# A fused graph layer on one core: a gate weight load issued later, row-sorting loads cut by row half, and two weight transforms in other batches

## The chip, the core and the metric

The kernel runs on one core of one Trainium2 chip, in float32. The time is the device time of one execution in microseconds (us); the figure given is the median of several executions. Engines are called PE (TensorE, matrix products and transposes), DVE (VectorE), ACT (ScalarE), POOL (GpSimd) and SP (SyncE, which only issues DMAs here). A DMA is issued by SP, ACT or POOL, each with a queue of its own, and moved by 16 DMA engines that all queues share.

## The reference

One layer of a graph network on 32 batches of 512 nodes with 256 features. With h = relu(layernorm(x)):

```python
h1 = relu(bn1(conv1(h)))                      # 1x1 convolution
x_conv = relu(bn2(conv2(h1)) + h)             # 17 taps along the nodes
s = h @ w_se.T + b_se                         # 3 columns
A = exp(-|s_n - s_m|^2) * adj                 # 512 x 512 for each batch
x_nmp = A @ relu(h @ w_msg.T + b_msg)
gi = concat(x_conv, x_nmp) @ w_ih.T + b_ih
gh = h @ w_hh.T + b_hh
r, z = sigmoid(gi_r + gh_r), sigmoid(gi_z + gh_z)
n = tanh(gi_n + r * gh_n)
out = x + (1 - z) * n + z * h
```

## The kernel before, in words

The 17-tap convolution is done in the frequency domain: the nodes of a batch are cut into windows of 64, transformed to 80 rows (40 "units" of two rows), multiplied by transformed weights, and turned back. A window transform serves 16 batches at once, so the 32 batches are two groups of 16, and the work comes in five stages in order of time:

1. the first part of group 0 (0 to 158 us): normalise, transpose, 1x1 convolution and window transform of batches 0 to 15, and in between the transform of the convolution's weights;
2. the nodes of group 0 (158 to 433): affinities, messages and aggregation, and the products of units 0 to 35;
3. the first part of group 1 (433 to 550): batches 16 to 31, with the four left-over units 36 to 39 of group 0 fitted in at its start;
4. the nodes of group 1 (550 to about 821);
5. the gates of all batches, in pairs (from 829).

The order inside a stage is written out by hand: each engine runs its instructions, and each queue issues its DMAs, in the program's order, so an instruction that waits holds all that stands behind it on the same engine. Buffers come from pools, and a load into a buffer waits until the last reader of the earlier content is done. PSUM has 8 banks used in turn.

What the change and the prediction's steps touch:

- `load_rows` (L196 to 199) loads a weight matrix of 256 rows so that partition 32g + i holds the rows 64g + i and 64g + 32 + i. It serves w1 (`load_w1`, into a buffer of 8 rows of which it uses 2), the message weights `wmsg` (256 columns, and 3 columns of the embedding `w_seT`), and two of the three gate weight matrices. It issues four DMAs of 32 partitions.
- `load_x` (L201) loads one batch of x, 512 KB. In `first_part` (L1126 on) batch b + 3 is loaded at the start of batch b's turn, by SP for the first three and by POOL from the fourth on. Three buffers.
- `statistics` (L375 to 381): mean and variance by DVE, then rstd by a power on POOL. `normalise` (L394 on DVE, L392 on ACT for one batch): xn. `transpose_h`: xn to PSUM by PE (L402, called phT), to hT by DVE (L406) with relu, and a store to DRAM by SP (L407, hd). `conv1`: PE (L422, pc), DVE (L425), ACT (L426). `windows_to_freq`: PE (L437, px), ACT copies (L440).
- Weights of the convolution: `load_taps` (L333, L334) loads an eighth of the taps in five DMAs; two buffers. There are 32 steps `weights_to_freq`, four for each eighth. One step is four groups of matmuls (L346, pw), each into a bank of its own, copies of them by ACT (L356) and DVE (L354), and after every second step four stores by SP (L360, wd). `between(b)` hands out the steps to the slots of each batch: n of them in batch b, at most three. Batch 0 has 2, batch 1 none, batches 6 and 11 three, all others two. The first stands after the transposes, the second after the 1x1 convolution, a third after the window transform. The load of the next eighth is put in front of the second step of each even batch from 2 to 12, on POOL, and it can start only when the eighth two places earlier is used up.
- `load_vectors` (L236) and `vectors` (L242 to 254): the bias and normalisation vectors, loaded in batch 5 and worked on by POOL in batch 6.
- The left-over units (L1408 to 1412). `prepare` loads a unit's weights if they are not there (L448, wt, 512 KB) and has POOL add up their two rows (L453, wsum) and the two rows of the factor (L466, both); `product` multiplies (L486, py), the third product needing wsum and both. The list `left` holds five lists of steps, and `first_part` runs one of them at each of its first five calls of `fill()`, among the work for batches 16 to 18. In the second list stands `combine.pop(0)`, which is the load of w_hh (768 KB, by `load_rows` on POOL's queue).
- `combine_weights` adds up the gate weights; its further steps run one in each batch from batch 18 on (`between` of group 1), the first arithmetic on w_hh at 460.60. The load of w_ih's columns for the convolved features goes through `load_rows` on SP's queue at 492.

Of the kernel before, what the change touches and what calls it, by code (L numbers as in the profile page):

```python
# [15 lines left out]
P = 128  # L16
# [134 lines left out]
def gnn_layer(  # L151
# [15 lines left out]
    nc = tc.nc  # L167
# [4 lines left out]
    DC = D // P  # L172
    NC = N // P
    G = 3 * D
    W = N // V
    GB = P // W
# [16 lines left out]
    X, ADJ, XN, HT, HQ, H1, MSG, A, NMP, ST, SL, SR = ({} for _ in range(12))  # L193
    XP, HP, NP, CP, YT, RZ, NT, OUT, AT, TS, MS = ({} for _ in range(11))

    def load_rows(dst, src, queue):  # L196

        for g in range(4):
            queue.dma_start(dst[32 * g : 32 * (g + 1)], src[64 * g : 64 * (g + 1)].rearrange("(e i) o -> i e o", e=DC))

    def load_x(b, queue=nc.sync):  # L201
        X[b] = pools["ahead" if b == GB else "first"].tile([P, NC, D], FP, tag="x", name=f"x_{b}", bufs=1 if b == GB else 3)
# [18 lines left out]
    at, cols, n = {}, {}, 0  # L221
# [1023 lines left out]
    @contextmanager  # L1245
    def phase(*names, bufs=1):
        with ExitStack() as stack:
            for name in names:
                pools[name] = stack.enter_context(tc.tile_pool(name=name, bufs=bufs, reuse_waits="tile"))
            yield  # L1250

    with tc.tile_pool(name="freq", bufs=1) as fpool:
        def freq_tile(g):
            return fpool.tile([P, DC, L, P], FP, tag="xf", name=f"xf_{g}")

        with phase("first", "gen"):
            gen = pools["gen"]
            per = N // D
            steps = [partial(weights_to_freq, gen, pc, i) for pc in range(QI // PI) for i in range(0, PI, per)]

            X[0] = pools["first"].tile([P, NC, D], FP, tag="x", name="x_0", bufs=3)
            for queue, c0, c1 in ((nc.sync, 0, 1), (nc.scalar, 1, 2), (nc.sync, 2, NC)):
                queue.dma_start(X[0][:, c0:c1, :], x[0, c0 * P : c1 * P, :].rearrange("(c p) d -> p c d", p=P))
            load_w1()
            load_x(1)
            load_taps(gen, 0, nc.sync)
            nc.sync.dma_start(taps, nc.inline_tensor(taps_np, name="dft_taps").ap())
            nc.sync.dma_start(fwd, nc.inline_tensor(fwd_np, name="dft_fwd").ap())

            def between(b):  # L1270
                if 1 <= b <= len(load_weights):
                    load_weights[b - 1]()

                n = (2, 0, *(3 if b in (6, 11) else 2 for b in range(2, GB)))[b]
                mine = [[steps.pop(0)] for _ in range(n)]
                if b % 2 == 0 and b // 2 + 1 < QI // PI:
                    mine[b > 0].insert(0, partial(load_taps, gen, b // 2 + 1))
                return (mine[0], mine[1:]) if b == 0 else mine

            with tc.manual_schedule():  # L1280
                xf = first_part(0, freq_tile, between)


        LEFT = 4

        def nodes(g, xf, units, last, following=()):


            b1 = (g + 1) * GB
            pw = pools["pw"]  # L1290
            todo = [b1 - 1, b1 - 2] + list(range(g * GB, b1 - 2))
            loads = [u for u in (*units, *following) if (g, u) not in WT]
            stores = []

            def load_units(n):
                for _ in range(n):
                    if loads:
                        load_unit(g, loads.pop(0))

            def flush():  # L1300
                while stores:
                    stores.pop(0)()

            def multiply(u):
                flush()
                product(pw, g, u, xf, stores)
                if u + 2 in units:
                    prepare(pw, g, u + 2, xf)
                load_units(1)

            load_adj(todo[0], 0)
            load_units(3 - sum((g, u) in WT for u in units))
            message(todo[0])
            load_adj(todo[1], 1)
            load_h(todo[3])
            features(todo[0])
            for step in message_sums(todo[0]):
                step()
            message(todo[1], [0])
            factors(todo[0])  # L1320
            by_chunks(todo[2])
            message(todo[1], [1])
            features(todo[1])
            exponents(todo[0])
            turn(todo[0], [0, 1])
            masked(todo[0], [0, 1])
            turn(todo[0], [2, 3])
            masked(todo[0], [2, 3])
            prepare(pw, g, units[1], xf)
            for step in affinity_sums(todo[0]):  # L1330
                step()
            for i, b in enumerate(todo):
                mine = spread(units, i, last) if i < last else []
                more = todo[i + 1 : i + 5]
                seven = i <= last

                def bring():
                    if len(more) > 1:
                        message(more[1])
                        features(more[1])  # L1340

                def ahead():
                    if len(more) > 2:
                        load_adj(more[1], i % 2)
                    if len(more) > 3:
                        load_h(more[3])

                if len(more) == 2:
                    load_adj(more[1], i % 2)
                flush()  # L1350
                if g + 1 < NG and i == GB // 2:
                    load_x(b1)
                if g + 1 < NG and i == 3 * GB // 4:
                    statistics(b1)
                if i > 0:
                    ahead()
                if more:
                    factors(more[0])
                if i == 0:
                    bring()  # L1360
                for u in mine[:1]:
                    multiply(u)
                if i == 0:
                    ahead()
                if i > 0:
                    bring()
                if not seven:
                    aggregate(b, [0])
                if more:
                    turn(more[0], [0, 1])  # L1370
                    exponents(more[0])
                    masked(more[0], [0, 1])
                for u in mine[1:2]:
                    multiply(u)
                if more:
                    turn(more[0], [2, 3])
                    masked(more[0], [2, 3])
                if seven:
                    aggregate7(b)
                else:  # L1380
                    aggregate(b, [1])
                if len(more) > 2:
                    by_chunks(more[2])
                stores.append(partial(save_nmp, b))
                for u in mine[2:]:
                    multiply(u)
                if more and i + 1 <= last:
                    block_sums(more[0])
            flush()

        with phase("pw", "ahead"):
            with phase("seven", "nodes"):
                with tc.manual_schedule():
                    nodes(0, xf, range(UNITS - LEFT), GB, range(UNITS - LEFT, UNITS - LEFT + 2))
            with phase("first", "sums"):
                combine = combine_weights()

                def between(b):

                    if b == GB - 3:  # L1400
                        for u in range(3):
                            load_unit(1, u)
                    two = [partial(sum_unit, pools["pw"], 1, b - GB + 3)] if b - GB + 3 >= REAL else []
                    return combine[b - 2] if 1 < b <= len(combine) + 1 else [], two


                pw, (u0, u1, u2, u3) = pools["pw"], range(UNITS - LEFT, UNITS)
                left = [[partial(load_unit, 0, u2, pools["sums"]), partial(prepare, pw, 0, u1, xf)],  # L1408
                        [*combine.pop(0), partial(product, pw, 0, u0, xf), partial(prepare, pw, 0, u2, xf)],
                        [partial(product, pw, 0, u1, xf), partial(load_unit, 0, u3)],  # L1410
                        [partial(prepare, pw, 0, u3, xf), partial(product, pw, 0, u2, xf)],
                        [partial(product, pw, 0, u3, xf)]]
                prepare(pw, 0, u0, xf)
                with tc.manual_schedule():
                    xf = first_part(1, freq_tile, between, left)
            with phase("seven", "nodes"):
                with tc.manual_schedule():
                    nodes(1, xf, range(UNITS), GB - 3)
# [92 lines left out]
```

## Time and profile before

| what | us |
|---|---|
| median of 3 runs | 1765.37 (1764.47 to 1765.94) |
| the profiled execution | 1765.63 |
| its span, first to last instruction | 1763.9 |
| PE busy | 1747.9 |
| DVE, POOL, ACT busy | 1333.7, 1108.6, 673.6 |

The profile is of one execution, so its rows are read against 1765.63 and its span, not against the median. "Busy" counts an instruction from its start to its end; the granted clock of PE was 0.999. A row of the timeline gives the start, the length, the engine with its line and operation, what it writes and reads, the number of instructions that are merged in it, and in brackets the idle time before it with what ended it. A row of the waits gives the total, the number and the longest. The chain of waits gives start and length of each piece, followed back from the last instruction to what released it.

PE's busy share by stage, from the table of windows: 153.1 of 158, 274.2 of 275, 115.1 of 117, 365.7 of 366, and 839.8 of 848.

### The profile page before, as it was taken

What the parts mean: (1) busy time and instruction counts of PE and PEld (TensorE: products, weight loads), DVE (VectorE), ACT (ScalarE), POOL (GpSimd) and SP (SyncE); (2) the same over time, 40 slices, a digit from 0 to 9 for tenths busy, and PEclk for the clock granted to TensorE, in tenths of its full rate; (3) what the DMA queues carried; (4) which work ended last, traced back from release to release, by engine and by line L of the source; (5) the groups of instructions that cost most, each with busy time, mean ns of one, the idle gap of its engine ahead of it and who ended that gap; (6) DMA issues with size and microseconds to landing.
All of it is one profiled execution on the core that took longest, in us unless ns stands there. A gap on an engine that the chain in (4) does not pass through costs nothing.

```text
span 1763.9 us, 24496 instructions
## 1 busy us (share of the span) xinstructions
PE 1747.9 (99%) x8046; PEld 1352.5 (77%) x8046; DVE 1333.7 (76%) x2618; ACT 673.6 (38%) x1543; POOL 1108.6 (63%) x1089
## 2 busy tenths in 40 slices
PE   9999999999999999999999999999999999999998
PEld 6677888888898888886877787777877787778754
DVE  7885877887996777776587778777877688777867
ACT  4556554543446445444313232223223232323221
POOL 3431887788654787787767556755666556755551
PEclk9999999999999999999999999999999999999999
DMA  9999998985779898889423453335423552345333
GB/s 251 300 304 232 255 237 236 238 225 180 267 241 219 256 238 238 229 230 299 149 73 70 109 126 103 71 78 125 117 69 66 125 126 73 69 110 125 101 61 72
DMA packets 311170, 295.16 MB, mean 167 GB/s; under 512 B 146924, under 2 KB 240652, under 8 KB 310660
## 3 DMA queue, kind: packets, MB, share of 16 engines
q1 hardware_dynamic: 301108, 265.24, 56.9%
q0 software_dynamic: 6928, 26.65, 4.8%
q10 hardware_dynamic: 3008, 1.72, 0.3%
q8 instruction: 64, 1.05, 0.3%
q14 instruction: 62, 0.51, 0.1%
HBM read 194.39 MB, written 99.16 MB: 166 GB/s over the span
## 4 chain that ended last, share of the span: by engine, by line
PE 94%; DVE 2%; DMA 2%; issue 1%; POOL 1%; ACT 0%; SPq 0%; ACTq 0%; POOLq 0%; DVEq 0%
PE pg L879 29%; PE pn L896 16%; PE py L486 11%; PE pn L641 10%; PE pm L537 6%; PE pc L422 5%; PE pc L844 5%; PE px L437 4%; PE pd L579 2%; PE pw L346 2%; PE phT L402 1%; PE pg L896 1%; PE pz L896 1%; PE pn L624 1%; PE psr L561 1%
## 5 line engine op out<-in xcount | busy, mean ns | idle before, releaser
L453 POOL TENSOR_TENSOR wsum<-wt 128x512 f32<-128x512 f32 x76 | 108.4, 1426 | 95.4 <-DMA wt<-wd 45.4
L486 PE MATMUL py<-wt,xf 128*128 128x256 f32 x640 | 154.2, 384 | 1.7 <-DMA wt<-wd 1.7
L879 PE MATMUL pg<-te,sw 128*128 128x256 f32 x600 | 154.0, 379 | 0.0
L486 PEld LDWEIGHTS py<-wt,xf 128*128 128x128 f32 x640 | 117.1, 190 | 36.8 <-issue 19.7
L870 ACT ACTIVATE rz<-rz,brz 128x256 f32<-128x256 f32 x180 | 86.2, 504 | 145.6 <-DVE rz L885 145.5
L589 DVE TENSOR_TENSOR A<-A,at 128x512 f32<-128x512 f32 x124 | 130.3, 1089 | 1.6 <-ACT A L585 1.5
L879 PEld LDWEIGHTS pg<-te,sw 128*128 128x128 f32 x600 | 114.0, 190 | 15.5
L879 PE MATMUL pg<-tn,sw 128*128 128x256 f32 x480 | 123.2, 379 | 0.0
L879 PE MATMUL pg<-hn,sw 128*128 128x256 f32 x480 | 123.2, 379 | 0.0
L896 PE MATMUL pn<-tn,sw_n 128*128 128x512 f32 x256 | 120.3, 592 | 0.0
L422 PE MATMUL pc<-w,hT 128*128 128x256 f32 x512 | 117.5, 382 | 0.8 <-DVE hT L406 0.8
L537 PE MATMUL pm<-wmsg,hq 128*128 128x259 f32 x512 | 117.5, 381 | 0.0
L1041 ACT ACTIVATE pn<-nt,vech 128x512 f32<-128x512 f32 x45 | 31.1, 692 | 218.5 <-DVE nt L1038 139.1
L422 PEld LDWEIGHTS pc<-w,hT 128*128 128x128 f32 x512 | 94.7, 190 | 23.6 <-issue 7.2
L782 POOL TENSOR_TENSOR tn<-hn 128x512 f32<-128x512 f32 x64 | 87.2, 1381 | 35.6 <-PE pn L896 35.6
L537 PEld LDWEIGHTS pm<-wmsg,hq 128*128 128x128 f32 x512 | 96.5, 189 | 14.7
L879 PEld LDWEIGHTS pg<-hn,sw 128*128 128x128 f32 x480 | 91.1, 190 | 18.3 <-PE pn L896 3.3
L879 PEld LDWEIGHTS pg<-tn,sw 128*128 128x128 f32 x480 | 91.2, 190 | 12.4
L885 DVE TENSOR_TENSOR ct<-pg,ct 128x256 f32<-128x256 f32 x180 | 74.5, 414 | 31.9 <-PE pg L879 21.6
L896 PEld LDWEIGHTS pn<-tn,sw_n 128*128 128x128 f32 x256 | 48.6, 190 | 61.2 <-issue 50.7
L381 POOL TENSOR_TENSOR rstd<-rstd,minus_half 128x4 f32<-128x4 f32 x32 | 33.4, 1042 | 97.5 <-DVE rstd L380 97.4
L844 PEld LDWEIGHTS pc<-back,yt 128*128 128x128 f32 x640 | 92.7, 190 | 1.3 <-issue 0.5
(227 smaller groups left out, 4425.0 us busy)
## 6 DMA issues: line engine op xcount, KB each, us to landing
wt<-wd SPq DMA_DIRECT2D x80, 512.0 KB, 7.7
adj<-in_adj_dram SPq DMA_DIRECT2D x128, 256.0 KB, 6.8
wd<-wst SPq DMA_DIRECT2D x64, 320.0 KB, 5.9
yd<-y SPq DMA_DIRECT2D x76, 256.0 KB, 5.1
yt<-yd SPq DMA_DIRECT2D x30, 640.0 KB, 6.1
hd<-hT SPq DMA_DIRECT2D x32, 512.0 KB, 4.7
nd<-nmp SPq DMA_DIRECT2D x32, 512.0 KB, 3.1
xb<-in_x_dram SPq DMA_DIRECT2D x128, 128.0 KB, 5.7
```

The lines of the kernel that those rows point to most:

```text
L422: nc.tensor.matmul(p[:, j, :], HT[b][:, ic, c * P : (c + 1) * P], w1[:, ic, :], start=(ic == 0), stop=(ic == DC - 1))
L453: nc.gpsimd.tensor_tensor(t, WT[g, u][:, 0], WT[g, u][:, 1], op=ALU.add)
L486: nc.tensor.matmul(dst, v[:, ic, :], w[:, ic, :], start=(ic == 0), stop=(ic == DC - 1))
L537: nc.tensor.matmul(p[:, : D + NS], hq[:, ic, c * P : (c + 1) * P], wmsg[:, ic, :], start=(ic == 0), stop=(ic == DC - 1))
L589: nc.vector.tensor_mul(A[b][:, mc, :], EXP.pop((b, mc)), AT.pop((b, mc)))
L641: nc.tensor.matmul(bk, left[:, k, :], right[:, k, :], start=(first and k == 0), stop=(k == 1), skip_group_check=True)
L782: nc.gpsimd.tensor_tensor(dst[:, k], x[:, k], y[:, k], op=op)
L844: nc.tensor.matmul(bk[:, t0:t1], YT[p][:, j, c, oc * P : (oc + 1) * P], back[:, n : n + t1 - t0], start=(c == 0), stop=(c == len(spans) - ...
L870: nc.scalar.activation(at(dst), at(src), AF.Sigmoid, bias=brz[:, o : o + 1], scale=sign)
L879: nc.tensor.matmul(bk, SW["hk"][:, k, s, :], c if k == 2 else hn[:, k], start=(onto is None and k == 0), stop=(k == K3 - 1), skip_group_ch ...
L885: nc.vector.tensor_tensor(at(dst), at(x), at(y), op=op)
L896: nc.tensor.matmul(bk[:, t], weight(q, k, o), terms[k][q][:, t], start=(first and i == 0), stop=(i == len(ks) - 1), skip_group_check=True)
```

## The change

It has four parts. (1) `load_rows` issues two DMAs of 128 partitions, one for each half of a group's rows, in place of four of 32 partitions with both halves. (2) The first batch of x is loaded in four pieces of one chunk, by SP and ACT in turn, in place of three pieces of one, one and two chunks. (3) The batches with three transform steps are 12 and 14 in place of 6 and 11. (4) `combine.pop(0)`, the load of w_hh, moves from the front of the second list of `left` to the end of the third, behind the load of unit 39.

```diff
     def load_rows(dst, src, queue):
 
-        for g in range(4):
-            queue.dma_start(dst[32 * g : 32 * (g + 1)], src[64 * g : 64 * (g + 1)].rearrange("(e i) o -> i e o", e=DC))
+        rows = src.rearrange("(g e i) o -> g e i o", g=4, e=DC)
+        for e in range(DC):
+            queue.dma_start(dst[:, e], rows[:, e])
...
             X[0] = pools["first"].tile([P, NC, D], FP, tag="x", name="x_0", bufs=3)
-            for queue, c0, c1 in ((nc.sync, 0, 1), (nc.scalar, 1, 2), (nc.sync, 2, NC)):
-                queue.dma_start(X[0][:, c0:c1, :], x[0, c0 * P : c1 * P, :].rearrange("(c p) d -> p c d", p=P))
+            for c in range(NC):
+                (nc.sync if c % 2 == 0 else nc.scalar).dma_start(X[0][:, c, :], x[0, c * P : (c + 1) * P, :])
...
-                n = (2, 0, *(3 if b in (6, 11) else 2 for b in range(2, GB)))[b]
+                n = (2, 0, *(3 if b in (12, 14) else 2 for b in range(2, GB)))[b]
...
                 left = [[partial(load_unit, 0, u2, pools["sums"]), partial(prepare, pw, 0, u1, xf)],
-                        [*combine.pop(0), partial(product, pw, 0, u0, xf), partial(prepare, pw, 0, u2, xf)],
-                        [partial(product, pw, 0, u1, xf), partial(load_unit, 0, u3)],
+                        [partial(product, pw, 0, u0, xf), partial(prepare, pw, 0, u2, xf)],
+                        [partial(product, pw, 0, u1, xf), partial(load_unit, 0, u3), *combine.pop(0)],
                         [partial(prepare, pw, 0, u3, xf), partial(product, pw, 0, u2, xf)],
                         [partial(product, pw, 0, u3, xf)]]
```

By the order of instructions on each engine, the w_hh load stands on POOL behind the wsum and both of unit 38 and the rstd of batch 18, in front of the load of batch 19; on SP, PE, DVE and ACT only the steps of parts (1) to (3) move.

## The prediction

> **What bounds the kernel now.** I read the page's busy table first, then the list of what TensorE (PE) waited for, then the chain of work and the engines' timelines at the places the diff touches.
>
> ```profile
> PE 1747.9 (99%) x8046; PEld 1352.5 (77%) x8046; DVE 1333.7 (76%) x2618; ACT 673.6 (38%) x1543; POOL 1108.6 (63%) x1089
> ```
>
> PE is busy for 1747.9 of 1763.9 us: the whole idle time is 16 us, and the edits change no matmul. So each part can only move waits of PE. The longest:
>
> ```profile
> PE row L1144 <- DVE fr L313: 1.9, 1, 1.9
> PE py L486 <- DMA wt<-wd: 1.7, 1, 1.7
> PE phT L402 <- DVE xn L394: 1.0, 1, 1.0
> ```
>
> The second is what the moved gate load may touch. Around it the PE timeline, then POOL's:
>
> ```profile
> 444.81 1.04 PE L402 MATMUL phT<-ident,xn 128*128 128x128 f32 x8
> 447.59 1.97 PE L486 MATMUL py<-wt,xf 128*128 128x256 f32 x8 [1.74 <-DMA wt<-wd]
> 449.67 1.13 PE L486 MATMUL py<-wsum,both 128*128 128x256 f32 x4
> 450.64 1.04 PE L402 MATMUL phT<-ident,xn 128*128 128x128 f32 x8
> ```
>
> ```profile
> 439.32 2.20 POOL L199 DMA_DIRECT2D w<-in_w_hhT_dram  x4
> 441.53 1.28 POOL L453 TENSOR_TENSOR wsum<-wt 128x512 f32<-128x512 f32 x1
> 442.76 0.73 POOL L466 TENSOR_TENSOR both<-xf 128x256 f32<-128x256 f32 x1
> 443.60 1.03 POOL L381 TENSOR_TENSOR rstd<-rstd,minus_half 128x4 f32<-128x4 f32 x1
> 444.60 0.82 POOL L203 DMA_DIRECT2D x<-in_x_dram  x1
> 447.62 1.26 POOL L453 TENSOR_TENSOR wsum<-wt 128x512 f32<-128x512 f32 x1 [2.20 <-DMA wt<-wd]
> ```
>
> The last left-over unit's weights (512 KB) were issued at 435.76 and took 11.7 us to land; PE stood 1.74 us for them, and 0.25 us more for the sum that POOL makes of them. The gate load of 768 KB goes out in between.
>
> The third place is batch 6 of group 0. The chain there:
>
> ```profile
> 59.56 5.53 DMA vec<-in_vecs_dram
> 67.56 0.99 POOL rstd L381
> 69.95 0.61 DVE h L425
> 71.72 0.57 ACT wst L356
> 72.33 2.12 PE pw L346 x6
> ```
>
> The late bias vectors hold POOL, behind them rstd, behind that VectorE's (DVE) normalisation and evictions, and at last the third transform (pw) finds no free bank: 2.06 us (72.33 to 74.39) where the chain lists 1.03 for one elsewhere.
>
> **What the Trainium skill says.** "DMA: Bandwidth & Descriptors", section "Why a DMA increments its semaphore by 16 and not by 1": a DMA is spread over the largest number of engines, up to 16, that divides the slowest dimension of both sides. The old row-sorting load has 32 partitions outermost on both sides, so 16 engines; the new one's source is (4 groups, 32 rows, columns), so 4. Nothing in the trace of before shows a load of this shape. Same page, "Queues, rings and completion order": each queue has a ring per engine, used in order, and an engine takes turns between queues. The trace agrees in kind: the gate load went out on POOL's queue, the unit's weights on SP's, and the latter took 11.7 us where the median of their 80 is 7.7. "PSUM — Partial Sum Buffer", "PSUM: the matmul accumulator": 8 banks; one transform needs four, and the 2.06 us above is the wait for their emptying.
>
> **The change part by part.** All against the profiled execution: 1765.63 us, span 1763.9, so 1.73 outside it; that run is 0.26 above the median 1765.37. The rate of one DMA engine: 363 GB/s moved in 440 to 445, by 16: 22.7 GB/s.
>
> 1. First loads. x[0]'s last 256 KB become 128 KB on SP and 128 KB on ACT: ACT's third issue costs 0.46, which its table load hides (1.28 from 1.68, needed at 4.62); statistics of the last chunk start at 5.6 in DVE's order, and a load on this queue took 3.7, so about 5.3: nothing. w1 (256 KB) in two DMAs saves SP two issues of 0.43, so all behind them start 0.9 earlier. But if on four engines, each carries 64 KB in place of 16: 48 KB more, 2.2 us. Net +1.3 for what lies behind on those engines. x[1] was issued at 3.58, landed 6.4 later at 9.98, and DVE took it at 10.15 with no wait: up to +1.1 us on the chain, which runs through DVE until 33. Zero if these were not the last engines to finish. I take +0.4.
>
> 2. Message weights (w_msg, 256 KB, at 17.83): again 48 KB more per engine; in 24 to 34 the rate was 291 GB/s, 18.2 an engine, so 2.7 us. x[5], issued at 27.84, landed 6.4 later (34.2) and was used at 34.29. DVE then is up to 2.6 late in a batch in which it has 0.77 + 0.45 idle; the rest delays ACT's evictions and the next transposes by up to 1.5. By 50 to 54 the queue has run thin, so the bias vectors don't feel it. I take +0.6, ends 0 and 1.5. The 3-column load is 3 KB in all and only saves SP two issues: nothing, SP waits for transforms there.
>
> 3. Third transform out of batch 6. Its matmuls (1.03) come back later. Without it the transposes stand at 72.33. ACT's three evictions from 71.72 end at 72.3, 72.8 and 73.3, so the two transposes end at 73.3; the next transform needs the third of these, DVE's (71.74) and the first two of ACT's px copies (73.14 on): it ends at 74.3 where before it ended at 76.44. 2.1 earlier with 1.03 less work: -1.0 (ends -0.3, if DVE becomes the wait, and -1.3).
>
> 4. Third transforms in batches 12 and 14 instead of 6 and 11. The one in batch 11 costs: 119.32 to 122.57 is 3.25 for work of 1.03 + 0.87 + 1.03: 0.32 of waiting for banks. Twice that less once: +0.3; the second has no transposes behind it. I take +0.2. With it its store moves: the store of step 30 comes after batch 14's third slot, some 3 us later on SP's queue; behind it the load of hT (issued 149.6, 5.4 to land, used at 165.1: covered by 10 us) and the mask load adj, which PE reaches through the 0.56 us wait at 179.42. +0.2, ends 0 and 0.8.
>
> 5. New waits on POOL. With the extra step gone, the tap loads in batches 8, 10 and 12 wait for that batch's second transform, as in batches 2, 4 and 6 now (4.81 us of POOL at 51.59). Behind them on POOL: the next batch's x and the next rstd. In batch 4 rstd went 1.3 us late (DVE done 53.8, POOL 55.17) and PE had no wait. x came 1.65 late at 62.62, inside the vectors' stall. DVE has 1.4 idle or more in each of batches 8 to 11, so nothing; +1 if two delays meet.
>
> 6. Gate load behind the left-over units. On POOL it moves past wsum, both and rstd, two issues in place of four: 2 x 0.55. The unit's weights then share with nothing of POOL's and land before 445.85. Next late is POOL itself: rstd ends 444.63, gate issues to 445.7, x[19] to 446.6, wsum 1.26, both 0.77: 448.6. So the unit's third product starts 1.1 earlier. After it the transposes wait for xn of batch 18, which DVE ends at 449.5 to 450.1: -0.8 is kept. But x[19] now stands behind the gate load. A free x load took 3.9 us (the shortest here): 1.4 of it transfer, 2.5 fixed. Each gate piece of 384 KB on four engines is 98 KB each, 4.3 us: the second, issued at 445.2, lands at 452.0, x[19] 1.4 behind it at 453.4. Statistics of batch 19 stood at 451.87; DVE has no idle time there, so xn ends 1.5 later (457.95), and the transposes that started at 457.14 go 0.8 late; at the highest rate in that stretch (462 GB/s) 0. I take +0.4. The 768 KB at 492 on SP: 8.7 us on four engines, x and hd there have over a batch (6.5 us) of room or share by turns: nothing.
>
> Sum: +0.4 + 0.6 - 1.0 + 0.2 + 0.2 + 0.4 = +0.8: 1766.4 for the profiled execution, 1766.2 for the median.
>
> **The rivals.** (a) The loads spread over 16 engines after all: parts 1 and 2 cost nothing, the boundary keeps its 0.8: -1.0 + 0.4 - 0.8 = -1.4, 1764.0. For it: gate loads of 192 KB landed in 6.6 to 7.8 and nothing shows four. Against: the source's shape. (b) Slower: both gate pieces land on the same four engines, 197 KB each, 8.7 us, so x[19] lands at 457.2, 5.3 late, and PE loses 4.6 instead of 0.4 at the transposes of batch 19: +5.0, 1770.4. It decides as soon as x[19] lands after 452.6, and costs one for one from there, as DVE is 99% busy. Against: a queue that takes the next engines in turn. (c) The change doesn't free the unit's weights, because SP's own queue holds them (four loads of 512 KB in 2 us): 1.0 of part 6 stays lost, 1767.2.
>
> **How the numbers follow.** The sum 0.55 (its own range 1764.6 to 1767.8), (a) 0.20, (b) 0.20, (c) 0.05. A measurement here tells 0.2% (3.5 us) from no change. Slower than 1768.9: most of (b) and a little of the sum's tail, 0.20. Faster than 1761.8: only with (a) and all lower ends, 0.03. Same 0.77. The range takes in (a)'s middle and half of (b): 1763.5 to 1770.0.
>
> **What would show it.** Right: no DMA wait of PE at L486, third transform gone from 72 with the next one ending near 74.3, DVE waiting for x near 10, 34 and 452. Wrong: x landings as before (then (a)); DVE idle by 4 or more at 452 (then (b)); PE waits anew in batches 8 to 13 (part 5 mis-sized).

## The result and the profile after

The changed kernel takes 1779.44 us, median of 6 runs (1775.70 to 1782.66); the kernel before took 1765.25 in the same session (6 runs, 1764.29 to 1766.90). The ratio is 1.0079, 95% interval 1.0069 to 1.0090: 13.9 us slower (12.2 to 15.9). The forecast was 1766.2, its range 1763.5 to 1770.0. The profiled execution is the fastest of the six, 1775.70 with a span of 1773.9, 10.0 more than before. The trace shows where these 10.0 went. The median loses some 4 us more, of which there is no trace; a fastest run 2.3 to 3.7 below the median is also what the kernel before shows in its longer series of 19 to 50 runs, so this need not be a further loss.

The busy table of the page after, the line that answers to the first one of the prediction:

```profile
PE 1752.1 (99%) x8046; PEld 1356.0 (76%) x8046; DVE 1334.5 (75%) x2618; ACT 674.0 (38%) x1543; POOL 1107.1 (62%) x1087
```

The same 8046 matmuls, but PE is *busy* 4.2 us longer than before (1747.9), and idle 21.8 us in place of 16.0. So 5.8 of the 10.0 are waits, and 4.2 are matmuls that took longer. The prediction had looked only for waits.

What PE waited for, after (total, times, longest):

```profile
PE phT L403 <- DVE xn L395: 5.2, 2, 4.9
PE pc L423 <- DVE hT L407: 4.2, 2, 3.7
PE row L1145 <- DVE fr L314: 1.9, 1, 1.9
PE py L487 <- POOL both L467: 1.1, 1, 1.1
```

The wait for the left-over unit's weights (1.7 at L486 before) is gone, as meant. Two new ones, 3.7 and 4.9, stand for far more. The first is at the start. DVE's timeline before and after, then PE's before and after:

```profile
8.89 0.74 DVE L280 TENSOR_TENSOR w<-w_in,row 128x256 f32<-128x256 f32 x2
```

```profile
8.09 0.41 DVE L281 TENSOR_TENSOR w<-w_in,row 128x256 f32<-128x256 f32 x1
11.66 0.42 DVE L281 TENSOR_TENSOR w<-w_in,row 128x256 f32<-128x256 f32 x1 [3.15 <-DMA w_in<-in_w1T_dram]
12.00 0.68 DVE L407 TENSOR_SCALAR hT<-phT 128x512 f32<-128x512 f32 x1
```

```profile
10.29 3.72 PE L422 MATMUL pc<-w,hT 128*128 128x256 f32 x16 [0.49 <-DVE hT L406]
```

```profile
12.73 5.25 PE L423 MATMUL pc<-w,hT 128*128 128x256 f32 x16 [3.74 <-DVE hT L407]
17.92 1.12 PE L347 MATMUL pw<-w2p,taps 17*80 17x512 f32 x8
18.97 1.09 PE L403 MATMUL phT<-ident,xn 128*128 128x128 f32 x8
```

The second half of w1 arrives at 11.66; before, both halves were scaled at 8.89 without a wait. PE waits 3.74, and its 16 products then take 5.25 us where they took 3.72. The transposes of batch 1, at 14.97 before, start at 18.97.

The second place is the boundary of the groups. POOL's timeline after, then PE's, first the two rows of before that compare with those at 464.50 and 466.58, then after:

```profile
447.57 1.46 POOL L200 DMA_DIRECT2D w<-in_w_hhT_dram  x2
449.02 0.82 POOL L204 DMA_DIRECT2D x<-in_x_dram  x1
449.86 1.28 POOL L454 TENSOR_TENSOR wsum<-wt 128x512 f32<-128x512 f32 x1
```

```profile
457.14 1.04 PE L402 MATMUL phT<-ident,xn 128*128 128x128 f32 x8
458.02 3.62 PE L422 MATMUL pc<-w,hT 128*128 128x256 f32 x16
```

```profile
451.93 1.13 PE L487 MATMUL py<-wsum,both 128*128 128x256 f32 x4 [1.08 <-POOL both L467]
452.90 1.04 PE L403 MATMUL phT<-ident,xn 128*128 128x128 f32 x8
453.77 3.62 PE L423 MATMUL pc<-w,hT 128*128 128x256 f32 x16
457.23 2.34 PE L438 MATMUL px<-fwd,h 128*128 128x160 f32 x16
464.50 2.29 PE L403 MATMUL phT<-ident,xn 128*128 128x128 f32 x8 [4.93 <-DVE xn L395]
466.58 5.23 PE L423 MATMUL pc<-w,hT 128*128 128x256 f32 x16
471.65 2.34 PE L438 MATMUL px<-fwd,h 128*128 128x160 f32 x16
```

The third product at L487 starts 2.26 later than before, in a pipeline that was 3.27 late until here: 1.0 us won. Then x[19], issued at 449.02, is used at 460.83, after 6.23 us of DVE's waiting; PE idles 4.93, and the transposes and products behind it take 2.29 and 5.23 in place of 1.04 and 3.62. From 471.65 on everything is about 10 late, to the end of the span.

| place (start of a PE step, after minus before) | us late |
|---|---|
| transposes of batch 1 | 4.00 |
| products of batches 1 to 6 | 4.13 |
| products of batches 7 to 10 | 1.91 |
| products of batch 11 | 3.15 |
| last products of stage one | 3.64 |
| transposes of batch 16 | 3.27 |
| products of batch 17 | 2.26 |
| products of batch 19 | 10.18 |
| end of the span | 10.0 |

### The profile page after: what moved, and what is told of

Its sections match the earlier page's. It is cut to its first block, busy times and chain, and to the rows that moved or that the text cites. A ratio compares the mean times of both kernels' runs of the same rounds, so it can differ in the third digit from the quotient of the medians.

```text
span 1773.9 us, 24475 instructions
## 1 busy us (share of the span) xinstructions
PE 1752.1 (99%) x8046; PEld 1356.0 (76%) x8046; DVE 1334.5 (75%) x2618; ACT 674.0 (38%) x1543; POOL 1107.1 (62%) x1087
## 4 chain that ended last, share of the span: by engine, by line
PE 95%; DVE 2%; DMA 1%; issue 1%; POOL 0%; ACT 0%; ACTq 0%; POOLq 0%; SPq 0%; DVEq 0%
PE pg L880 28%; PE pn L897 16%; PE py L487 11%; PE pn L642 10%; PE pm L538 6%; PE pc L423 5%; PE pc L845 5%; PE px L438 4%; PE pd L580 2%; PE pw L347 2%; PE phT L403 1%; DMA x<-in_x_dram 1%; PE pg L897 1%; PE pz L897 1%; PE pn L625 1%
## 5 line engine op out<-in xcount | busy, mean ns | idle before, releaser
L487 PE MATMUL py<-wt,xf 128*128 128x256 f32 x640 | 154.2, 384 | 0.0
L487 PEld LDWEIGHTS py<-wt,xf 128*128 128x128 f32 x640 | 117.1, 190 | 34.9 <-issue 19.7
```

The source lines that it names most:

```text
L487: nc.tensor.matmul(dst, v[:, ic, :], w[:, ic, :], start=(ic == 0), stop=(ic == DC - 1))
```

## The experiments

The theory: a row-sorting load in two DMAs has a source whose outermost dimension is 4, runs on 4 of the 16 DMA engines, and lands late; w1 and the gate load are then waited for, the latter by way of x[19], which is queued behind it. The rivals: the gate load's new place alone costs; the slots of the transforms; the half-row form of the loads. Each time is a ratio to the kernel before on the same chip, with its interval in us; "in the profile" is the lateness of PE's steps against the profile of before.

**rows_only**: `load_rows` of the change, nothing else.

> The kernel before with nothing changed but the row-sorting loads (two DMAs over 128 partitions whose source has 4 as its outermost dimension). Theory (such a DMA runs on 4 of the 16 engines): the first weights land some 4 us late again and TensorE waits about 4 us at 8 to 13 us; the gate load at its old place, on four engines, lands 9 to 12 us after its issue at 439 instead of 7, the next x, issued 5 us after it, some 2 us late: +4 to +8 in all, 1769 to 1773. Rival (the loads do no harm where they were, the new place of the gate load does it): 1765 to 1766. Rival (slots or taps): 1765.

Measured 1.0052 (1.0038 to 1.0066): +9.2 us (6.7 to 11.6), above the top of what the theory gave (8). In the profile PE waits 2.10 for hT behind w1 and is 4.8 late from batch 1, then slow again in batches 2 to 5 with few waits; at batch 19 it waits 2.18. The loads do harm at their old places too.

**after_old_rows**: the changed kernel, with these lines of before back.

```
-        rows = src.rearrange("(g e i) o -> g e i o", g=4, e=DC)
-        for e in range(DC):
-            queue.dma_start(dst[:, e], rows[:, e])
+        for g in range(4):
+            queue.dma_start(dst[32 * g : 32 * (g + 1)], src[64 * g : 64 * (g + 1)].rearrange("(e i) o -> i e o", e=DC))
```

> The changed kernel with the old four-DMA row-sorting loads put back; x[0] in four pieces, slots 12 and 14 and the new place of the gate load stay. Theory (four engines): no wait on the first weights, x of batch 19 lands near 453 to 455; left are -0.8 of the x[0] pieces, -1.2 of batch 6, +1.2 of batch 10, -0.5 of slot 11, -1.0 at the gate load with 0 to +2 back for x of batch 19: 1763 to 1765. Rival (the place of the gate load in front of x[19] is what costs, with any spread): 1768 to 1773. Rival (slots): over 1766.

Measured 1.0015 (1.0008 to 1.0022): +2.6 us (1.4 to 3.9). Most of the loss goes with the loads, but what is left is no gain, where the theory had 0 or less: the rival on the slots has a share (its places are under steps 3 and 5 below). x[19] is waited for 0.64 by DVE here, with the gate load at its new place.

**after_rows8**: the changed kernel with eight DMAs for each load, one half-row of 32 partitions each.

```
+        for g in range(4):
+            rows = src[64 * g : 64 * (g + 1)].rearrange("(e i) o -> e i o", e=DC)
+            for e in range(DC):
+                queue.dma_start(dst[32 * g : 32 * (g + 1), e], rows[e])
```

> The changed kernel with each row-sorting load in eight DMAs of 32 partitions and one half-row each: the packets and the half-row form of the change, an outermost dimension of 32, and more issues than before instead of fewer. Theory (the spread decides): waits on the first weights and on x of batch 19 mostly gone, but four issues more of 0.43 to 0.55 us on SP's queue ahead of x[1] and on POOL ahead of x[19]: 1764 to 1768. Rival (the half-row form, or the strides of the write, is what is slow): 1776 to 1781 as in the change. Rival (fewer and larger DMAs in themselves were worth something, and it is all the place): 1772 and more.

Measured 1.0065 (1.0053 to 1.0078): +11.5 us (9.3 to 13.8), far above what was expected. By place: w1 is there when DVE scales it (8.0), pieces of the gate load land in 2.5 to 4.7 us, x[19] is waited for 0.39. So half-rows are not slow. The time goes to the issues themselves; the waits of PE, then POOL's timeline:

```profile
PE py L488 <- POOL both L468: 3.5, 1, 3.5
PE pw L348 <- DMA w2p<-in_w2T_dram: 2.1, 1, 2.1
```

```profile
451.62 4.07 POOL L201 DMA_DIRECT2D w<-in_w_hhT_dram  x8
455.68 0.81 POOL L205 DMA_DIRECT2D x<-in_x_dram  x1
```

Eight issues hold POOL 4.07 us in front of the left-over unit's sums. SP's eight for w1 make the first taps late, and its eight for w_msg take 8.00 us (2.31 for the four of before), behind which DVE waits 4.81 for an x. The total tells nothing on the spread, the places do.

**after_rows2**: four DMAs of 64 partitions, source with 2 outermost.

```
+        rows = src.rearrange("(h g e i) o -> h e g i o", h=2, g=2, e=DC)
+        for h in range(2):
+            for e in range(DC):
+                queue.dma_start(dst[64 * h : 64 * (h + 1), e], rows[h, e])
```

> The changed kernel with each row-sorting load in four DMAs of 64 partitions whose source has 2 as its outermost dimension. Theory (the engines are as many as the outermost dimension divides, and always the same ones): twice the bytes on half the engines: first weights another 5 to 8 us later, the gate load 17 us and more, x[19] behind it: 1787 to 1805. Rival (successive DMAs take the next engines in turn): four DMAs on eight engines, better than the change, 1768 to 1776. Rival (the number of DMAs decides): as before, 1765.

Measured 1.0163 (1.0149 to 1.0177): +28.8 us (26.3 to 31.2). The same bytes in as many DMAs as before: the outermost dimension decides. w1 is used at 12.3 and 13.8, x[19] at 469.5. But the gate pieces of 192 KB landed in 8.3 to 12.6 us, not far from those of 384 KB (9.1 and 10.3 in the changed kernel). If the first run on two engines and the second on four, both put 96 KB on an engine; had all four pieces gone to one pair of engines, each would have carried 384 KB, an estimate of 17 us of transfer at the 22.7 GB/s of the prediction. So they did not all go to one pair. That POOL's successive DMAs take other engines in turn fits, but no run shows which engines they used.

**slots_only**: `b in (12, 14)` for `b in (6, 11)`, nothing else.

> The kernel before with nothing changed but the third weight transforms, in batches 12 and 14 in place of 6 and 11. Theory (the tap load of POOL, queued ahead of an x load, waits longer for the transforms that free its buffer; x of batch 12 is late): TensorE loses 1.2 at batch 11 and gains nothing or 1.2 at batch 6: 0 to +2.0, 1764 to 1766. Rival (the prediction on record: -1.0 at batch 6, +0.2 later, no new wait): -0.8 to -0.4, below 1764.

Measured 1.0005 (0.9994 to 1.0015): +0.9 us (-1.1 to 2.6). The time doesn't tell, the profile does: 1.36 earlier from batch 7 (1.03 of it work moved away), 1.01 back at batch 11, and over stage one 0.13 later in all. POOL's timeline there, and DVE's at batch 12:

```profile
88.55 2.17 POOL L333 DMA_DIRECT2D w2p<-in_w2T_dram  x4 [5.54 <-PE pw L346]
90.70 0.62 POOL L334 DMA_DIRECT2D w2p<-in_w2T_dram  x1
91.31 0.80 POOL L203 DMA_DIRECT2D x<-in_x_dram  x1
```

```profile
100.68 1.41 DVE L375 BATCH_NORM_STATS2 stats<-x 128x6 f32<-128x256 f32 x4 [2.76 <-DMA x<-in_x_dram]
```

The tap load waits 5.54 for the transform that frees its buffer, x[12] is issued behind it, and DVE waits 2.76.

**slots_6_14**: `b in (6, 14)`.

> The kernel before with the third weight transform of batch 11 alone moved, to batch 14; that of batch 6 stays. Theory (it is the removal from batch 6 that makes the tap load of batch 8 wait, and x of batch 12 behind it late): no new wait at batch 11 (there +1.0 with both moved), -1.3 at batch 12 and +0.9 at batch 14: -0.4 in the profile, 0 in the time. Rival (the tap load waits whatever is moved): +1.0 at batch 11 again.

Measured 1.0001 (0.9993 to 1.0009): +0.2 us (-1.2 to 1.6), nothing. The same stretch of POOL:

```profile
85.79 2.90 POOL L333 DMA_DIRECT2D w2p<-in_w2T_dram  x4 [0.29 <-PE pw L346]
88.69 0.61 POOL L334 DMA_DIRECT2D w2p<-in_w2T_dram  x1
89.30 0.80 POOL L203 DMA_DIRECT2D x<-in_x_dram  x1
```

The tap load waits 0.29, DVE's statistics of batch 12 not at all, and PE is no later at batch 11 than at batch 10. The slot taken out of batch 6 makes the wait, not those put in.

**x0_only**: x[0] in four pieces, nothing else.

> The kernel before with nothing changed but x[0] in four pieces. Theory (one more issue on SP's queue ahead of the x loads of batches 1 and 2): -0.1 to -0.8 at the first transposes and 0.6 lost again by batch 2: -0.2 to +0.6. Rival (prediction on record): nothing. Rival (the pieces are what made the changed kernel's first transposes 0.8 earlier, and that is kept): -0.8.

Measured 1.0000 (0.9989 to 1.0011): nothing, as the prediction had it. The 0.8 that the changed kernel's first transposes came earlier is no gain of the pieces: they came 0.1 to 0.9 earlier in most of these profiles, with or without them.

**gate_only**: `*combine.pop(0)` moved from the second list of `left` to the end of the third, nothing else.

> The kernel before with nothing changed but the place of the gate load (old four-DMA form). Theory (with sixteen engines x of batch 19 is hardly late): -1.0 at the third product of the left-over unit, 0 to 0.3 back at batch 19: -0.4 to -1.0. Rival (any 768 KB ahead of x[19] makes TensorE wait): +2 to +7.

Measured 1.0006 (0.9994 to 1.0018): +1.1 us (-1.1 to 3.2). No loss of several us by the place alone; the gain of 0.4 to 1.0 can't be seen in the time. In the profile PE is 0.26 earlier at batch 18 than at batch 16, and 0.09 over the whole stretch: with the weights in time, it waits 1.83 for POOL's sums instead, which stand behind four issues of 2.20 us.

**gate_two_new**: gate_only, with the change's two-DMA form for the gate loads and for these alone (a second helper).

> The kernel before with the new place of the gate load and two DMAs for this load alone; first weights and message weights as before. Theory (four engines carry it, x of batch 19 is queued behind it on the same engines): TensorE waits 4 to 5 us for xn of batch 19 and runs some 2.8 us slower after it, less 1.0 won: +5 to +8, 1769 to 1772. Rival (in the changed kernel the wait at batch 19 came from the lateness of the whole pipeline): -1 to +1.

Measured 1.0036 (1.0023 to 1.0048): +6.4 us (4.1 to 8.5), as the theory had it. Here the pipeline is on time until batch 18 (1.68 early), so it isn't lateness from before. The statistics of batch 19 on DVE, then the stretches of 6 us (busy times, then granted clock of PE, DMA share, GB/s):

```profile
457.64 1.41 DVE L381 BATCH_NORM_STATS2 stats<-x 128x6 f32<-128x256 f32 x4 [6.98 <-DMA x<-in_x_dram]
```

```profile
452.00:458.00 6.00, 3.62 (x23) 3.23 (x21) 0.36 (x2) 0.00 (x0) 0.00 (x0) 1.00 0.86 277
458.00:464.00 6.00, 2.68 (x10) 2.18 (x11) 5.93 (x20) 1.15 (x3) 1.81 (x2) 0.53 0.42 145
464.00:470.00 6.00, 6.00 (x33) 5.42 (x32) 5.95 (x18) 2.25 (x7) 4.44 (x8) 0.90 0.57 199
```

PE waits 5.69; in the 6 us around the end of the wait its granted clock is 0.53, then 0.90.

**gate_two_old**: the two-DMA gate loads at the old place.

> The kernel before with the gate load alone in two DMAs, at its old place. Theory (four engines, but five to eight us earlier than in the changed kernel): x of batch 19 is late by less, +1 to +4, against +6.4 at the new place. Rival (the place doesn't matter): +6 and more.

Measured 1.0019 (1.0011 to 1.0027): +3.4 us (1.9 to 4.8). Here the loss is elsewhere: x[19] is waited for only 0.51 by DVE, but PE waits 3.44 for the left-over unit's weights (1.74 before), and its next eight products take 3.54 us (1.97 before). The gate pieces themselves took 13.0 and 13.4 us to land, longer than at the new place.

**w1_two**: the two-DMA form for w1 alone.

> The kernel before with the first weights alone in two DMAs; all other loads as before. Theory (four engines): DVE waits 1.5 to 3 us for the second half near 10 to 12 us, TensorE waits 2 to 4 us for hT and runs up to 1.6 us slower after it: +3 to +5.5, 1768 to 1771. Rival (prediction on record: only x of batch 1 is late): +0.4.

Measured 1.0027 (1.0019 to 1.0035): +4.8 us (3.4 to 6.2). DVE waits 2.77 for the second half, used at 11.52; PE waits 3.35, its products take 5.41, and it is 4.00 late at batch 1.

**wmsg_two**: the two-DMA form for w_msg alone.

> The kernel before with the message weights alone in two DMAs. In the profile of the rows-only kernel TensorE lost 4.6 us between batches 2 and 6, in that of the changed kernel nothing. Theory (the message load makes x of batch 5 late only when it meets other late loads): 0 to +1.5. Rival (it costs by itself, on four engines): +2 to +5.

Measured 1.0006 (0.9996 to 1.0017): +1.1 us (-0.7 to 3.0): inconclusive. In the profile nothing changes until batch 6; then PE is 3.8 later in two batches, by products of 5.97 us at 78.12 after waits of no more than 0.74. What this has to do with the load isn't settled.

**gate_two_new_fill**: gate_two_new with 20 products more, into a bank that nobody reads, ahead of the transposes of batch 19.

> The kernel with the gate load at its new place in two DMAs, and 20 matmuls more (identity by the first weights, into a bank nobody reads) on TensorE ahead of the transposes of batch 19, which fill 4.5 us of its wait of 5.7. Theory (it is the idle stretch that makes TensorE's next matmuls slow): the wait shrinks to about 1.2, the transposes take 1.04 and not 2.29 us and the products 3.6 and not 4.5: 2 us less than without the fill, +4.2, about 1770. Rival (the slow matmuls have another cause, such as the loads that land then): still slow, +6.3.

Measured 1.0075 (1.0061 to 1.0089): +13.2 us (10.8 to 15.7). The fill missed its place, so this kernel doesn't test the theory. Its PSUM bank was still held by DVE, so it came after the wait and not in it:

```profile
459.60 11.88 PE L1238 MATMUL warm<-w,ident 128*128 128x256 f32 x40 [4.04 <-DVE hT L412]
471.32 1.04 PE L408 MATMUL phT<-ident,xn 128*128 128x128 f32 x8
472.19 3.62 PE L428 MATMUL pc<-w,hT 128*128 128x256 f32 x16
```

(A product shows as two instructions.) By the next kernel's fill (4.48 for 20 instructions) the 40 should take 9.0; they took 11.88. What comes first after the wait is slow here too, and the transposes, coming later, are not.

**gate_two_new_fill2**: the fill goes into the first px bank of batch 16, ahead of its own products.

```
                 p = bank(f"px_{b}_{ic}_{c0}")
+                if (b, ic, c0) == (GB, 0, 0):
+                    for _ in range(10):
+                        nc.tensor.matmul(p[:, :D], ident, w1[:, 0, :], start=True, stop=True)
```

> The kernel with the gate load at its new place in two DMAs, and 10 products more (identity by the first weights, into the first px bank of batch 16 before its own products overwrite it), which fill 4.5 us of the 5.7 that TensorE waits ahead of the transposes of batch 19. Theory (the idle stretch makes the next matmuls slow): the wait is 1.2 or less, the transposes of batch 19 take 1.04 and not 2.29 us, the products after them 3.6 and not 4.5: two us less than the +6.3 of the kernel without the fill, +4.2 in the profile. Rival (something else, such as the loads in flight, slows the matmuls): 2.29 and 4.5 again, +6.3.

PE's timeline and the stretches, as above:

```profile
453.38 4.48 PE L444 MATMUL px<-w,ident 128*128 128x256 f32 x20
457.69 2.34 PE L446 MATMUL px<-fwd,h 128*128 128x160 f32 x16
461.27 1.73 PE L408 MATMUL phT<-ident,xn 128*128 128x128 f32 x8 [1.24 <-DVE xn L400]
462.83 3.72 PE L428 MATMUL pc<-w,hT 128*128 128x256 f32 x16
```

```profile
458.00:464.00 6.00, 4.74 (x28) 3.78 (x28) 5.94 (x20) 1.19 (x3) 1.81 (x2) 1.00 0.43 141
464.00:470.00 6.00, 6.00 (x39) 5.65 (x38) 5.95 (x18) 2.26 (x7) 4.45 (x8) 1.00 0.58 203
```

x[19] is as late as before (used at 457.59), the loads in flight are the same (141 and 203 GB/s against 145 and 199), but the granted clock stays at 1.00 and the products take 3.72 (4.51 in gate_two_new). The transposes take 1.73, less than 2.29 and more than the 1.04 expected: DVE finishes the last of xn only at 462.18, while they run, so 0.7 of their length is no matter of the clock. From their start to the end of the products PE loses 2.09 in gate_two_new and 0.79 here: 1.3 less, not the 2 expected. The time doesn't show it: 1.0046 (1.0033 to 1.0059) is +8.1 us (5.8 to 10.4), no less than gate_two_new's +6.4, with intervals that overlap. So the link from the idle time to the clock is shown at this place of one profile, and not that the fill makes the kernel faster.

**gate_two_behind_x**: as gate_two_new, but the gate load one list later, so behind x[19] on POOL.

> The kernel with the gate load in two DMAs, moved once more, behind the issue of x of batch 19 and the last left-over unit's sums on POOL. Theory (on POOL's queue a load waits for those issued before it on its engines): x of batch 19 is free of it and on time; x of batch 20, issued right behind the gate load, is now the late one, by 0 to 4 us; +0 to +4 against the kernel before, less than the +6.4 of the load in front of x of batch 19. Rival (four engines under load delay all loads alike, whatever their order): +6 again.

Measured 1.0046 (1.0030 to 1.0062): +8.1 us (5.3 to 10.9), more than the 0 to 4 expected; the mechanism held and the size did not. DVE's two statistics:

```profile
449.92 1.39 DVE L381 BATCH_NORM_STATS2 stats<-x 128x6 f32<-128x256 f32 x4
...
463.50 1.41 DVE L381 BATCH_NORM_STATS2 stats<-x 128x6 f32<-128x256 f32 x4 [7.80 <-DMA x<-in_x_dram]
```

x[19], now ahead of the gate load, is in time without any wait; x[20], now behind it, is 7.80 late. The delay follows the order on POOL's queue. The gate pieces took 12.9 and 15.0 us to land here.

The parts run alone give w1 4.8, w_msg 1.1, gate loads at the new place 6.4, slots 0.9, x[0] 0.0: 13.2 together, and the whole change 13.9. With the gate loads at the old place, 4.8, 1.1 and 3.4 make 9.3, against the 9.2 of rows_only. Each part is known to 1 to 2 us, so that the sums meet so closely is in part luck.

## Why the prediction was wrong

That the new loads run on 4 engines fits every run, and the place of the larger loss was named; the sum made of them was wrong. Three steps failed: the first loads (1) and the gate load (6), by the rate of a DMA engine that they reckoned with, and the new waits on POOL (5). By its own steps:

1. *First loads, +0.4.* This step failed. It let only x[1] be late, by up to 1.1, and never asked whether w1 itself would be in time, though DVE scales it at 8.89. The loads of w1 in the trace of before (four DMAs of 64 KB; durations of the issues, first and last start, then landing), and after:

```profile
L199 SPq DMA_DIRECT2D w_in<-in_w1T_dram x4: 427/428/460, 1.7 to 3.1; - x4
...
DMA to landing us min/median/max: 3.1/3.3/3.6
```

```profile
L200 SPq DMA_DIRECT2D w_in<-in_w1T_dram x2: 562/646/729, 1.7 to 2.4; - x2
```

Before, each piece landed 3.1 to 3.6 us after its issue. After, the second half was issued 0.7 earlier, at 2.4, and was there at 11.66, 9.3 us later. If w1 ran on four engines, the 64 KB of w1 and 32 of x[0] on each took until 11.66: an estimate of 11 GB/s from 3.0 on (shortly after the second issue), half of the 22.7 that the step used. At 22.7 they would have been there at 7.3, in time, so asking for w1 would not have been enough: the rate is what failed. Why an engine gave only half isn't settled; x[1] is in the same queue. Measured: +4.00 in the profile of w1_two, +4.8 in its time.

2. *Message weights, +0.6.* 0 in the profile of the change (4.13 late from batch 1 to batch 6), +1.1 (-0.7 to 3.0) alone: not contradicted.

3. *Third transform out of batch 6, -1.0.* In the change PE wins 2.22 between batches 6 and 7, of which 1.03 is moved work: -1.2. In slots_only it is -0.3, and in after_old_rows +1.1. The three differ by when the bias vectors land, which the prediction had named as the cause of this wait. Times of POOL's second copy of them (vech) and of PE's products of batch 7:

| kernel | copy | products | between |
|---|---|---|---|
| before | 65.23 | 76.44 | 11.21 |
| slots_6_14 (batch 6 as before) | 65.15 | 76.36 | 11.21 |
| the change | 68.62 | 78.35 | 9.73 |
| slots_only | 64.70 | 74.43 | 9.73 |
| after_old_rows | 67.27 | 77.01 | 9.74 |

With the third transform gone the products follow the copy 1.48 sooner; 1.03 of it is moved work, so the step is worth -0.45, not -1.0. The rest is the copy's time against PE's products of batch 6, which is 0.75 earlier than before in the change, 0.1 later in slots_only and 1.5 later in after_old_rows. All other profiles fall on these two values within 0.03, but for wmsg_two (12.23), whose slow stretch lies there. What sets the landing of the vectors isn't settled.

4. *Slots in 12 and 14, +0.2 and +0.2.* In slots_only PE is 1.35 earlier at batch 12 (the slot that left batch 11, 1.03 of work), 0.97 later at batch 13 and 0.86 at batch 15, against 1.03 of work each: the new slots cost nothing beyond their work, and a little is won at 11. Neither +0.2 showed.

5. *New waits on POOL, nothing.* This step failed. It took batch 4 as its pattern, where the same wait of a tap load did no harm, and named "+1 if two delays meet". In batch 8 x[12] stands behind the tap load and is waited for: +1.24 in the change (batch 10 to 11), +1.01 in slots_only, 0 in slots_6_14. "DVE has 1.4 idle or more" covers a late rstd; it doesn't cover an x that is 2.8 to 3.0 late.

6. *Gate load, +0.4 (0.8 won, then lost again and 0.4 more).* This step failed by its size. The gain was there: 1.0 in the change. It needs the two issues: behind four (2.20 us of POOL for 1.46), in gate_only and after_old_rows, 0.26 and 0.36 are won. The loss was mis-sized: x[19] was to land at 453.4, the gate pieces in 6.8 us (4.3 of transfer and 2.5 fixed). In gate_two_new they took 9.5 and 10.9, and x[19] was used at 457.64; PE is 6.27 late after it, where +0.4 was forecast. Rival (b) had this size (x[19] at 457.2, 4.6 lost), but the landings speak against its mechanism: with both pieces on the same engines, in order, the second would land after the first by its whole transfer, 4.3 us or more by the step's own sum. w1's halves did come apart (the first by 8.09, the second at 11.66, for a third of these bytes); the gate's two pieces landed at most 2.2 apart. Each engine was slower than the 22.7 GB/s that is the mean of sixteen: 96 KB in 7.0 to 8.4 us beyond the fixed 2.5 is 12 to 14, an estimate from these landings. That x[19], spread over all engines, then ends with the slowest of them is argued, not shown.

What no step and no rival had is the second price of a wait: PE's next matmuls take longer. At w1 it is 1.5 us (5.25 for 3.72), at batch 19 2.9 (1.25 in the transposes, of which some 0.7 is the waiting for xn seen in gate_two_new_fill2, and 1.6 in the products): 4.4 by these rows, against the 4.2 that PE is busier on the page. "Costs one for one" in rival (b) was wrong. The Trainium skill states it ("TensorE: Matmul & The Clock Gate", section "What's actually happening"): after an idle window of about 3.4 us TensorE runs at half its clock until it has been busy for such a window. The runs agree in kind: 0.53 granted after 5.69 us of waiting and 1.00 with the wait filled. They don't agree on the length: waits of 2.10 and 2.18 in rows_only were followed by slow matmuls, one of 2.33 in after_rows2 was not.

Rival (a), all loads on sixteen engines, was to give 1764.0. That kernel was run: after_old_rows, 2.6 slower than before. Without the loads the change is not the gain of 1.4 that (a) summed. By the rows above, step 3 gives -0.45, step 4 about -0.5, step 5 +1.0 to +1.4 (1.43 in after_old_rows) and step 6 nearly nothing (0.09 in gate_only): 0 to +0.5. What the rest of the 2.6 is isn't settled; slots_only and gate_only alone measured +0.9 and +1.1, both with 0 inside the interval.

On the spread: "DMA: Bandwidth & Descriptors", section "Why a DMA increments its semaphore by 16 and not by 1", has it that a DMA of a hardware queue (SP's) takes the lowest-numbered engines, and one of a software queue (POOL's) the next ones in turn. The landings agree in kind: w1's halves came one after the other, the gate's pieces nearly together. So w1's two halves met on the same four engines, by that page, and the gate's two pieces did not; no run here shows which engines these are.

Open stays why the runs of one kernel spread as they do: 7.0 us for the six of the change, 2.6 for the six of before beside them, but 6.8 to 9.0 in the longer series of before, so it is no mark of the change. Slow stretches of PE come at other places in other kernels' profiles (batches 2 to 5 in rows_only, 6 to 8 in wmsg_two, after waits under 1 us), and one costs 2 us or more, so they may be the cause. That is argued, not shown.

## What to carry to other kernels

Before two DMAs replace four, write down the outermost dimension of both sides: a source with 4 outermost is, by the page that the prediction cites and by all that these runs show, a load on 4 engines, and its price is its own landing first, then that of each load queued behind it. In a kernel like this one, price a wait of PE of two us or more at its length plus up to 3 us of slow matmuls, and read the page's busy time with the count of matmuls: more time for the same count shows it. For each issue that now waits, name the loads behind it on its queue and when each is needed, batch by batch; that the same wait did no harm in another batch proves nothing.

## What the hardware showed that was not expected

- TensorE's clock after a wait: in a stretch of six us at its end a granted clock of 0.51 (the change, 464 to 470, after 4.93 us) and 0.53 (gate_two_new, 458 to 464, after 5.69), and 0.72 already after 2.10 and 2.18 us (rows_only, 12 to 18 and 464 to 470). The matmuls behind it lose 1.5 to 3 us. Ten products without use inside the wait (4.48 us) kept it at 1.00.
- A load on few engines was slower than its share of the whole: an estimated 11 to 14 GB/s for an engine with 64 to 96 KB of it (w1, and the gate at its new place), 9 to 10 with the gate at its old place, where the mean of sixteen is 22.7.
- Pieces of 192 KB on two engines took 8.3 to 12.6 us to land (after_rows2), of 384 KB on four 9.1 and 10.3 (the change) and 12.7 to 13.4 at the old place (rows_only, gate_two_old). On sixteen engines, by the same count, the 192 KB took 3.2 to 5.1 (gate_only) and 6.6 to 7.8 at the old place (before).
